# A diffusion transformer block on one core: ten of its sixteen MLP batches taken in pairs, with wider matmuls

## The chip, the cores and the metric

The kernel runs on 1 core of a Trainium2 chip. The metric is device time in microseconds (us) of one execution. Three executions were timed and one further execution was profiled. In the profile the engines are PE (matmul, with its weight loads shown apart as PEld), DVE, ACT and POOL; SP issues DMAs.

## The reference

One block with self-attention, cross-attention and an MLP over 16 batches of 256 tokens with 256 features. What the change touches is the end, the MLP (cut to it):

```python
        x = x + c_attn_out
        x_norm2 = modulate(_ln(x), shift_m, scale_m)
        h = jax.nn.gelu(x_norm2 @ W_mlp1 + b_mlp1)
        h = h @ W_mlp2 + b_mlp2
        x = x + gate_m[:, None] * h
        return x
```

The scale, shift and gate differ from batch to batch; the two weight matrices (256 x 1024 and 1024 x 256) are the same for all.

## The kernel before

The attention of all batches comes first, and takes the span's first three quarters. It stores each batch's stream to a DRAM buffer, `x2d`. The MLP follows, with the first batches' preparation already laid into the end of the attention.

**Precision.** Each f32 operand of a product is split into a high part (type fp32r) and a low part, high and low being `hi` and `lo`, or `hh` and `hl`. A product is three matmuls for each slice of 128 in the contraction: high by high, high by low, low by high (`mm3`, `mm3_tok`).

**A batch's preparation.** `mlp_load` fetches the batch from `x2d` (SP). `mlp_bias` adds a row on POOL (`x<-x,cb`). `mlp_stats` takes mean and variance on DVE (`st_m`, `mv_m`, `rs_m`) and raises to the power -1/2 on POOL (`rs_m<-rs_m,mhalf`). `mlp_apply` normalizes on DVE, in two halves (`xn_m`). Below these three together are the norm. `mlp_T` is the turn: PE transposes `xn_m` into PSUM (`psT_m`, four transposes), DVE scales and shifts it (`xTf_m`), ACT makes `hi` (or a DVE copy, for the batches in the list `'DV'`), and DVE makes `lo`. `mlp_residual` fetches the gate rows (`gm`) and adds one to the stream on DVE (`xmg`).

**A chunk.** The 1024 hidden features are taken 256 at a time, so a batch has four chunks (b, 0) to (b, 3). A chunk is three stages. `mlp_first` (lines 747 to 758) is the first product into one PSUM bank (`ph`): two slices of 128 features, each six matmuls with 256 moving columns, the batch's tokens. `mlp_gelu` (760 to 773) reads that bank on ACT, twice for each half: `hf` in f32 and `hh` in fp32r; POOL subtracts them into `hl`. `mlp_second` (775 to 789) multiplies by W2 into the bank pair `sp` or `st`, 12 matmuls with 256 moving columns. With the last chunk it ends the batch: DVE multiplies both halves by the gate (`mt`), adds the residual (`y`), and SP stores.

**The order.** It is written out by hand in the loop from line 1122. At chunk i the program issues gelu of chunk i+1, the turn of a batch if one is due, the first product of chunk i+2, the second product of chunk i-1, then the norm, residual or load that is due. PE, DVE, POOL and SP keep the program's order, each as its own queue; ACT does so up to chunk `'AP'`, 23, and the built order is the program's after it too. Before the change, batch b+1 is turned at (b, 0), batch b+2 is normed at (b, 1), the residual of batch b is taken at (b, 2), and batch b+3 is loaded at (b, 3). The first two chunk positions of the loop are special and not touched.

Buffers: `hh` and `hl` have three each, `ph` two, `x` five, `xn` three.

Of the kernel before, what the change touches and what calls it, by code (L numbers as in the profile page):

```python
# [21 lines left out]
def pixart_block(  # L22
# [8 lines left out]
    B, N, H = x.shape  # L31
# [3 lines left out]
    NT = N // P  # L35
    KC = H // P
    MLP = W_mlp1.shape[1]
    NF = MLP // P
# [13 lines left out]
                return tc.keep_in_program_order(i) if self.on else i  # L52
            return issue

    E_ = {'M': ((-17, -12, -10, -1, 1), (0, 3, 4, 7, 9), (8, 11, 13, 15)), 'CUT': 8, 'LN': {'s': 'pool', 'c': 'pool', 'q': 'pool'}, 'ON': (1, 1, 1), 'L0': -16, 'L1': 1, 'S0': -7, 'A0': 0, 'T0': 1, 'H': (7, 11, 14, 15), 'S1': 5, 'A1': 7, 'L2': 9, 'T1': 9, 'S2': 32, 'AP': 23, 'DV': (0, 1), 'HP': (1, 0), 'BZ': {}, 'AV': {1: [(1, 2), (1, 3)], 9: [(0, 0), (0, 1)]}, 'AHEAD': (0, 0, 0, 0, 0, 2), 'W1P': [(-9, 1), (-8, 1), (-7, 1), (-6, 1), (-5, 1), (-5, 5), (-4, 1), (-4, 3), (-4, 5), (-3, 1), (-3, 3), (-3, 5), (-2, 1)], 'W2P': [(-4, 7), (-3, 0), (-3, 4), (-3, 6), (-3, 7), (-2, 2), (-2, 4), (-2, 6), (-1, 0), (-1, 1)], 'XP': 1, 'IL': 1, 'MF': 0, 'SH': 4, 'RAMP': 1, 'HA': 1, 'MP': 16, 'W': (7, 1, 0, 0), 'PRE': 'z0qp z0kp load rest ld2 one0 silu b12 brow L0a turn L0b b4 L0d scale T0t sc1 hik lok T0h T0l b4 shift b4 hiq L1a L1b bk loq K0a K0b K0x0 K0x1 K0y0p K0y1p L1d T1t K0l T1h K0l0 K0l1 Q0a Q0m bq Q0h Q0x0 Q0y0p Q0x1 Q0y1p T1l Q0l Q0l0 Q0l1 z1kp z1qp K1a K1b hiv lov Q1a Q1b K1x0 K1x1 K1y0 K1y1 K1l K1l0 K1l1 Q1x0 Q1x1 Q1y0 Q1y1 Q1l Q1l0 Q1l1 L2a L2b L2c V0a V0b bv b5 ld3', 'SL': {(-1, 0): 'V1a', (-1, 1): 'T2t T2h T2p vone z2kp z2qp', (-1, 2): 'V1b', (-1, 3): 'rest', (-1,4): 'M0 rest one1 ld4', (-1, 5): 'K2a L3a', (-1, 6): 'K2m L3b L3p L3c', (-1, 7): 'd3 one2 rest', (0, 0): 'd6 rest', (0, 1): 'rest', (0, 2): 'd3', (0, 4): 'rest', (1, 0): 'rest', (1, 2): 'rest', (1, 4): 'rest', (30, 0): 'd3', (30, 1): 'd2', (30, 2): 'd3', (30, 5): 'd3', (31, 1): 'd2'}}

    PE = InOrder(nc.tensor, True)
    ACT, DVE, POOL, SP = (InOrder(e, True) for e in (nc.scalar, nc.vector, nc.gpsimd, nc.sync))

    const = ctx.enter_context(tc.tile_pool(name="const", bufs=1))  # L60
    work = ctx.enter_context(tc.tile_pool(name="work", bufs=2))
# [23 lines left out]
    big = [const.tile([P, 2, 8, N], F32R, name=f"big{i}") for i in range(3)]  # L85
# [6 lines left out]
    BMOD, BQKV, BQC, BKVC, BM1 = 0, 12, 18, 20, 24  # L92
# [5 lines left out]
    def tok(ap, b):  # L98
        return ap[b].rearrange("(t p) h -> p t h", p=P)
# [5 lines left out]
    brow = const.tile([32, P], F32, name="brow")  # L105
# [20 lines left out]
    sc1 = const.tile([P, 2, 2, B], F32, name="sc1")  # L126
    bT = const.tile([P, 32], F32, name="bT")
# [5 lines left out]
    st = psum.tile([P, 2, 512], F32, tag="st", name="st", bufs=1)  # L133
    sp = psum.tile([P, 2, 512], F32, tag="s", name="s", bufs=1)
# [35 lines left out]
    ts = [work.tile([P, 2, KC, H], F32, tag="pt", name=f"wf{i}", bufs=5) for i in range(3)]  # L170
# [552 lines left out]
    def mlp_T(b):  # L723

        m = M[b]
        pst = ps_gen(f"psT_m{b}", SHORT)
        for f in range(KC):
            for t in range(NT):
                PE.transpose(pst[:, f * N + t * P:f * N + (t + 1) * P],
                             m.ln.xn[:, t, f * P:(f + 1) * P], ident)  # L730
        y = work.tile([P, KC, N], F32, tag="y", name=f"xTf_m{b}", bufs=2)
        hi, lo = (Wkc, Wqc)[b % 2]
        for f in range(KC):
            DVE.tensor_scalar(y[:, f], pst[:, f * N:(f + 1) * N], sc1[:, 1, f, b:b + 1],
                              cpT[:, 6 + f, b:b + 1], ALU.mult, ALU.add)
# [24 lines left out]
    def mlp_gelu(b, c):  # L760
        ph = M[b].h.pop(c)
        hf = work.tile([P, 2, N], F32, tag="pt", name=f"hf_{b}_{c}", bufs=5)
        hh = work.tile([P, 2, N], F32R, tag="qkh", name=f"hh_{b}_{c}", bufs=3)
        hl = work.tile([P, 2, N], F32R, tag="qkl", name=f"hl_{b}_{c}", bufs=3)
        for dst in (hf, hh):
            if b == 0:
                ACT.activation(dst, ph, AF.Gelu_apprx_tanh)
                continue
            for j in range(2):
                f = BM1 + 2 * c + j  # L770
                ACT.activation(dst[:, j], ph[:, j], AF.Gelu_apprx_tanh, bias=bT[:, f:f + 1])
        POOL.tensor_tensor(hl, hf, hh, ALU.subtract)
        M[b].hT[c] = (hh, hl)

    def mlp_second(b, c):
        m = M[b]
        hT = m.hT.pop(c)
        if c == 0:
            m.po = [(sp, st)[b % 2][:, t, :H] for t in range(NT)]
        for t in range(NT):  # L780
            mm3_tok(m.po[t], hT, t, [W2[0][:, 2 * c:2 * c + 2], W2[1][:, 2 * c:2 * c + 2]],
                    kn=2, start=(c == 0), stop=(c == NCH - 1))
        if c == NCH - 1:
            t1 = work.tile([P, NT, H], F32, tag="t1", name=f"mt_{b}")
            for t in range(NT):
                DVE.tensor_tensor(t1[:, t], m.po[t], m.g[:, 0], ALU.mult)
            y = work.tile([P, NT, H], F32, tag="x1", name=f"y_{b}", bufs=5)
            DVE.tensor_tensor(y, m.xg, t1, ALU.add)
            SP.dma_start(tok(out, b), y)


    W1P, W2P = E_['W1P'], E_['W2P']
    W1 = [wself[:, 8 * i:8 * i + 8].rearrange("p (k c) h -> p k (c h)", k=KC) for i in range(2)]
    W2 = [big[2][:, 0], big[2][:, 1]]
# [301 lines left out]
    for n in range(-1, nu):  # L1096
        ACT.on = E_['ON'][0] or n >= nu - 1
        for k in range(8):
# [7 lines left out]
            for q in (2 * k, 2 * k + 1):  # L1106
# [6 lines left out]
    pst = iter([lambda: o.turn(1), lambda: o.norm(1),  # L1113
                lambda: (o.aT.turn(), o.aT.high()), o.aT.low,
                lambda: o.proj(0), lambda: o.proj(1), lambda: (o.end(), o.add(), o.store())])
    chunks = [(b, c) for b in range(B) for c in range(NCH)]
    mlp_first(*chunks[4])
    mlp_gelu(*chunks[0])
    next(pst)()
    mlp_first(*chunks[5])  # L1120
    next(pst)()
    for i, (b, c) in enumerate(chunks):
        ACT.on = i < E_['AP']
        if i + 1 < len(chunks):
            mlp_gelu(*chunks[i + 1])
        if c == 0 and 0 < b < B - 1:
            mlp_T(b + 1)
        if i > 3 and i + 2 < len(chunks):
            mlp_first(*chunks[i + 2])
        if i > 0:  # L1130
            mlp_second(*chunks[i - 1])
        for _, f in zip(range(1), pst):
            f()
        if c == 1 and 2 < b + 2 < B:
            mlp_bias(b + 2)
            mlp_stats(b + 2)
            mlp_apply(b + 2)
        if c == 2:
            mlp_residual(b)
        if c == 3 and b + 3 < B:  # L1140
            mlp_load(b + 3)
    mlp_second(*chunks[-1])


# [46 lines left out]
```

## Time and profile before

| what | value |
|---|---|
| median of three runs | 805.61 us (803.01 to 806.17) |
| the profiled execution | 804.78 us |
| its span, first to last instruction | 803.0 us |
| PE, PEld busy | 97%, 82% |
| DVE, ACT, POOL busy | 74%, 73%, 58% |
| granted clock of PE | 1.0 |
| matmuls | 9455 |

The first row is the time that counts; the second is the execution from which every duration here is taken. Busy shares are over the whole span. A PE that is busy 97% has little room, but matmuls overlap in the pipeline: the distance between starts tells what one costs, not its duration. In a timeline row the columns are the start in us, the length in us, the engine, the line, the operation with output and inputs, the count, and in brackets the idle time before it with what ended that. In a row of waits they are the engine that waited and its tile, what it waited for, the total in us, the number of times, and the longest. All instructions carry line 51, that of a recording helper, so one goes by the tiles' names.

### The profile page before, as it was taken

The numbers are of one execution on the slowest core, as the hardware profiler recorded it, in microseconds if no ns is written. First come the engines' busy times: TensorE is split into PE (matmuls) and PEld (weight loads), VectorE is DVE, ScalarE is ACT, GpSimd is POOL, SyncE is SP. The second block draws the span as 40 slices with busy tenths as digits, with TensorE's granted clock in tenths as the row PEclk, the third lists the DMA queues.
The fourth block names the chain that finished last, engine by engine and source line by source line (L and its number), as shares of the span: only waits on it lengthen the run. The fifth ranks groups of instructions, "written<-read, shape, count | busy, mean of one in ns | idle before, by whom it ended". The sixth has DMA issues, their size and how long they took to land.

```text
span 803.0 us, 23712 instructions
## 1 busy us (share of the span) xinstructions
PE 781.8 (97%) x9455; PEld 660.3 (82%) x9455; DVE 596.0 (74%) x1063; ACT 584.8 (73%) x1024; POOL 465.4 (58%) x405
## 2 busy tenths in 40 slices
PE   9999999999999999999999999999899999999997
PEld 8677777887887877878788788777669999999997
DVE  4787878888888888878887888777674656666662
ACT  3377887888887888878888788877666666666663
POOL 5745837475564647456364767654446666666653
PEclk9999999999999999999999999999999999999999
DMA  6553444345353444535444454534311322212211
GB/s 189 147 172 95 133 113 123 100 120 146 95 147 104 137 107 123 146 94 146 113 132 130 137 151 120 148 101 129 106 42 42 92 60 60 80 58 62 80 43 51
DMA packets 89938, 87.88 MB, mean 109 GB/s; under 512 B 9506, under 2 KB 85572, under 8 KB 89828
## 3 DMA queue, kind: packets, MB, share of 16 engines
q1 hardware_dynamic: 89364, 85.58, 37.7%
q8 instruction: 75, 1.23, 0.7%
q0 software_dynamic: 192, 0.52, 0.2%
q14 instruction: 35, 0.29, 0.1%
q10 hardware_dynamic: 272, 0.26, 0.1%
HBM read 26.97 MB, written 8.46 MB: 44 GB/s over the span
## 4 chain that ended last, share of the span: by engine, by line
PE 79%; DVE 9%; ACT 4%; POOL 3%; issue 3%; DMA 1%; ACTq 0%; POOLq 0%; SPq 0%
PE s L51 17%; PE o L51 14%; PE ph L51 11%; PE st L51 11%; DVE mx L51 7%; PE ps_qc L51 3%; PE ps_kc L51 3%; PE ps_q L51 3%; ACT pt L51 2%; PE ps_P_s L51 2%; PE ps_v_s L51 2%; PE ps_v_c L51 2%; PE psm L51 2%; PE ps_k L51 1%; PE ps_P_c L51 1%
## 5 line engine op out<-in xcount | busy, mean ns | idle before, releaser
L51 DVE TENSOR_REDUCE mx<-s 128x4 f32<-128x1024 f32 (+1 forms) x267 | 309.2, 1163 | 94.6 <-PE s L51 92.0
L51 ACT ACTIVATE pt<-st 128x1024 f32<-128x1024 f32 x252 | 257.0, 1020 | 40.3 <-PE st L51 34.1
L51 PE MATMUL s<-big 63*128 63x256 f32 (+1 forms) x1024 | 122.1, 309 | 6.5 <-DVE mx L51 3.6
L51 PE MATMUL o<-pt,v 128*32 128x256 f32 x2048 | 123.8, 382 | 0.0
L51 POOL TENSOR_TENSOR hl<-hf,hh 128x512 fp32r<-128x512 f32 x64 | 88.7, 1396 | 55.0 <-ACT hh L51 54.0
L51 PEld LDWEIGHTS s<-big 63*128 63x128 f32 (+1 forms) x1024 | 81.2, 185 | 41.6 <-DVE mx L51 19.0
L51 PE MATMUL st<-big 64*128 64x256 f32 (+1 forms) x1024 | 108.8, 284 | 4.9 <-ACT pt L51 4.9
L51 PEld LDWEIGHTS o<-pt,v 128*32 128x32 f32 x2048 | 60.0, 109 | 40.8
L51 PEld LDWEIGHTS st<-big 64*128 64x128 f32 (+1 forms) x1024 | 82.1, 186 | 9.3 <-ACT pt L51 7.5
L51 ACT ACTIVATE hf<-ph,bT 128x256 f32<-128x256 f32 x120 | 50.6, 474 | 27.8 <-PE ph L51 27.8
L51 ACT COPY oT<-o 128x512 f32<-128x512 f32 x63 | 37.0, 587 | 42.5 <-PE o L51 42.5
L51 ACT ACTIVATE hh<-ph,bT 128x256 fp32r<-128x256 f32 x120 | 50.5, 472 | 23.8 <-PE s L51 12.0
L51 POOL TENSOR_TENSOR xTl_c<-y_c,xTh_c 128x512 fp32r<-128x512 f32 x16 | 20.5, 1282 | 61.6 <-PE s L51 52.3
L51 POOL TENSOR_TENSOR xTl_as<-y_as,xTh_as 128x512 fp32r<-128x512 f32 x16 | 20.5, 1279 | 56.4 <-ACT y_as L51 56.4
L51 PE MATMUL ph<-wqch,wself 128*128 128x256 f32 x256 | 51.8, 285 | 0.0
L51 PE MATMUL ph<-wkch,wself 128*128 128x256 f32 x256 | 51.8, 286 | 0.0
L51 POOL TENSOR_TENSOR xTl_ac<-y_ac,xTh_ac 128x512 fp32r<-128x512 f32 x16 | 20.6, 1284 | 52.8 <-ACT y_ac L51 48.8
L51 PE MATMUL s<-big,hh 128*128 128x256 f32 x256 | 47.4, 282 | 0.0
L51 PE MATMUL st<-big,hh 128*128 128x256 f32 x256 | 47.2, 281 | 0.0
L51 DVE TENSOR_SCALAR xn_m<-x,mv_m,rs_m 128x256 f32<-128x256 f32 x32 | 38.4, 1238 | 11.4 <-POOL rs_m L51 11.4
L51 PEld LDWEIGHTS ph<-wqch,wself 128*128 128x128 f32 x256 | 42.0, 191 | 0.4 <-issue 0.4
L51 PEld LDWEIGHTS ph<-wkch,wself 128*128 128x128 f32 x256 | 41.9, 191 | 0.4
(223 smaller groups left out, 2381.0 us busy)
## 6 DMA issues: line engine op xcount, KB each, us to landing
big<-h_kc SPq DMA_DIRECT2D x64, 128.0 KB
big<-h_qc SPq DMA_DIRECT2D x64, 128.0 KB
big<-h_k SPq DMA_DIRECT2D x62, 128.0 KB
big<-h_q SPq DMA_DIRECT2D x62, 128.0 KB
big<-l_k SPq DMA_DIRECT2D x32, 128.0 KB
big<-l_q SPq DMA_DIRECT2D x32, 128.0 KB
c<-in_ctx_dram SPq DMA_DIRECT2D x16, 256.0 KB
g<-gd SPq DMA_DIRECT2D x16, 256.0 KB
```

The lines of the kernel that those rows point to most:

```text
L51: i = f(*a, **k)
```

## The change

Batches 4 to 13 become five pairs (4,5) to (12,13). A pair's `hi` and `lo` lie side by side in a part of `big[0]`, a tile that the attention has left by then, so that one matmul moves 512 columns, the tokens of both batches. A pair has eight chunks of 128 features, labelled (2p, 0) to (2p+1, 3): six wide matmuls, two gelu operations of 512 columns, one subtraction, and 12 matmuls of the second product, 256 columns each as before. Both batches of a pair end together, after its eighth chunk. The other batches keep their functions.

The preparation is moved: pairs turn batch v+2 at (v, 0), norm batch v+3 at (v, 1) and load batch v+4 at (v, 3). Between single batches and pairs the order is listed: norm 3 at (1, 1), 4 at (1, 3), 5 at (2, 1); turn 3 at (2, 0), 4 at (2, 2), 5 at (3, 0). The `hi` of batches 3, 4 and 5 is made on DVE. The last batch ends in two halves of 128 tokens, each multiplied, added and stored by itself. Which of `sp` and `st` a batch or pair accumulates in is chosen anew.

```diff
-    'DV': (0, 1)
+    'DV': (0, 1, 3, 4, 5)
...
         hi, lo = (Wkc, Wqc)[b % 2]
+        if 3 < b < B - 2:
+            q = b // 2 % 2
+            m.pair = [big[0][:, i, 4 * q:4 * q + 4].rearrange("p (k e) n -> p k (e n)", k=KC)
+                      for i in range(2)]
+            hi, lo = [w[:, :, b % 2 * N:b % 2 * N + N] for w in m.pair]
...
+    def mlp_end(b, ts=(slice(0, NT),)):
+        m = M[b]
+        t1 = work.tile([P, NT, H], F32, tag="t1", name=f"mt_{b}")
+        y = work.tile([P, NT, H], F32, tag="x1", name=f"y_{b}", bufs=5)
+        for s in ts:
+            for t in range(NT)[s]:
+                DVE.tensor_tensor(t1[:, t], m.po[t], m.g[:, 0], ALU.mult)
+            DVE.tensor_tensor(y[:, s], m.xg[:, s], t1[:, s], ALU.add)
+            SP.dma_start(tok(out, b)[:, s], y[:, s])
+
+    def two_first(p, f):
+        ph = ps_gen(f"ph2_{p}_{f}", LONG)
+        xT = M[2 * p + 1].pair
+        n = 0
+        for k in range(KC):
+            for a, b in ((0, 0), (0, 1), (1, 0)):
+                PE.matmul(ph, W1[a][:, k, f * P:(f + 1) * P], xT[b][:, k], start=(n == 0), stop=(n == 3 * KC - 1))
+                n += 1
+        M[2 * p].h[f] = ph
+
+    def two_gelu(p, f):
...
+        for dst in (hf, hh):
+            ACT.activation(dst.rearrange("p e n -> p (e n)"), ph, AF.Gelu_apprx_tanh,
+                           bias=bT[:, BM1 + f:BM1 + f + 1])
+        POOL.tensor_tensor(hl, hf, hh, ALU.subtract)
+
+    def two_second(p, f):
+        hT = M[2 * p].hT.pop(f)
+        for e in range(2):
...
+            for t in range(NT):
+                for n, (a, b) in enumerate(((0, 0), (0, 1), (1, 0))):
+                    PE.matmul(m.po[t], hT[a][:, e, t * P:(t + 1) * P], W2[b][:, f],
...
+        if f == NF - 1:
+            mlp_end(2 * p)
+            mlp_end(2 * p + 1)
...
+    chunks = [single(b, c) for b in range(4) for c in range(NCH)]
+    chunks += [double(p, f) for p in range(2, B // 2 - 1) for f in range(NF)]
+    chunks += [single(b, c) for b in range(B - 2, B) for c in range(NCH)]
+    turns = {(1, 0): [2], (2, 0): [3], (2, 2): [4], (3, 0): [5]}
+    norms = {(1, 1): [3], (1, 3): [4], (2, 1): [5]}
+    loads = {(0, 3): [3], (1, 0): [4], (1, 2): [5]}
+    for v in range(4, B - 2):
+        turns[v, 0] = [v + 2]
+    for v in range(3, B - 3):
+        norms[v, 1] = [v + 3]
+    for v in range(2, B - 4):
+        loads[v, 3] = [v + 4]
```

More of the change, by code (lines that the diff above doesn't have):

```diff
@@ L53, in __getattr__ @@
             return issue
-    E_ = {'M': ((-17, -12, -10, -1, 1), (0, 3, 4, 7, 9), (8, 11, 13, 15)), 'CUT': 8, 'LN': {'s': 'pool', 'c': 'pool', 'q': 'pool'}, 'ON': (1, 1, 1), 'L0': -16, 'L1': 1, 'S0': -7, 'A0': 0, 'T0': 1, 'H': (7, 11, 14, 15), 'S1': 5, 'A1': 7, 'L2': 9, 'T1': 9, 'S2': 32, 'AP': 23, 'DV': (0, 1), 'HP': (1, 0), 'BZ': {}, 'AV': {1: [(1, 2), (1, 3)], 9: [(0, 0), (0, 1)]}, 'AHEAD': (0, 0, 0, 0, 0, 2), 'W1P': [(-9, 1), (-8, 1), (-7, 1), (-6, 1), (-5, 1), (-5, 5), (-4, 1), (-4, 3), (-4, 5), (-3, 1), (-3, 3), (-3, 5), (-2, 1)], 'W2P': [(-4, 7), (-3, 0), (-3, 4), (-3, 6), (-3, 7), (-2, 2), (-2, 4), (-2, 6), (-1, 0), (-1, 1)], 'XP': 1, 'IL': 1, 'MF': 0, 'SH': 4, 'RAMP': 1, 'HA': 1, 'MP': 16, 'W': (7, 1, 0, 0), 'PRE': 'z0qp z0kp load rest ld2 one0 silu b12 brow L0a turn L0b b4 L0d scale T0t sc1 hik lok T0h T0l b4 shift b4 hiq L1a L1b bk loq K0a K0b K0x0 K0x1 K0y0p K0y1p L1d T1t K0l T1h K0l0 K0l1 Q0a Q0m bq Q0h Q0x0 Q0y0p Q0x1 Q0y1p T1l Q0l Q0l0 Q0l1 z1kp z1qp K1a K1b hiv lov Q1a Q1b K1x0 K1x1 K1y0 K1y1 K1l K1l0 K1l1 Q1x0 Q1x1 Q1y0 Q1y1 Q1l Q1l0 Q1l1 L2a L2b L2c V0a V0b bv b5 ld3', 'SL': {(-1, 0): 'V1a', (-1, 1): 'T2t T2h T2p vone z2kp z2qp', (-1, 2): 'V1b', (-1, 3): 'rest', (-1,4): 'M0 rest one1 ld4', (-1, 5): 'K2a L3a', (-1, 6): 'K2m L3b L3p L3c', (-1, 7): 'd3 one2 rest', (0, 0): 'd6 rest', (0, 1): 'rest', (0, 2): 'd3', (0, 4): 'rest', (1, 0): 'rest', (1, 2): 'rest', (1, 4): 'rest', (30, 0): 'd3', (30, 1): 'd2', (30, 2): 'd3', (30, 5): 'd3', (31, 1): 'd2'}}
@@ new lines, in pixart_block @@
+    E_ = {'M': ((-17, -12, -10, -1, 1), (0, 3, 4, 7, 9), (8, 11, 13, 15)), 'CUT': 8, 'LN': {'s': 'pool', 'c': 'pool', 'q': 'pool'}, 'ON': (1, 1, 1), 'L0': -16, 'L1': 1, 'S0': -7, 'A0': 0, 'T0': 1, 'H': (7, 11, 14, 15), 'S1': 5, 'A1': 7, 'L2': 9, 'T1': 9, 'S2': 32, 'AP': 23, 'DV': (0, 1, 3, 4, 5), 'HP': (1, 0), 'BZ': {}, 'AV': {1: [(1, 2), (1, 3)], 9: [(0, 0), (0, 1)]}, 'AHEAD': (0, 0, 0, 0, 0, 2), 'W1P': [(-9, 1), (-8, 1), (-7, 1), (-6, 1), (-5, 1), (-5, 5), (-4, 1), (-4, 3), (-4, 5), (-3, 1), (-3, 3), (-3, 5), (-2, 1)], 'W2P': [(-4, 7), (-3, 0), (-3, 4), (-3, 6), (-3, 7), (-2, 2), (-2, 4), (-2, 6), (-1, 0), (-1, 1)], 'XP': 1, 'IL': 1, 'MF': 0, 'SH': 4, 'RAMP': 1, 'HA': 1, 'MP': 16, 'W': (7, 1, 0, 0), 'PRE': 'z0qp z0kp load rest ld2 one0 silu b12 brow L0a turn L0b b4 L0d scale T0t sc1 hik lok T0h T0l b4 shift b4 hiq L1a L1b bk loq K0a K0b K0x0 K0x1 K0y0p K0y1p L1d T1t K0l T1h K0l0 K0l1 Q0a Q0m bq Q0h Q0x0 Q0y0p Q0x1 Q0y1p T1l Q0l Q0l0 Q0l1 z1kp z1qp K1a K1b hiv lov Q1a Q1b K1x0 K1x1 K1y0 K1y1 K1l K1l0 K1l1 Q1x0 Q1x1 Q1y0 Q1y1 Q1l Q1l0 Q1l1 L2a L2b L2c V0a V0b bv b5 ld3', 'SL': {(-1, 0): 'V1a', (-1, 1): 'T2t T2h T2p vone z2kp z2qp', (-1, 2): 'V1b', (-1, 3): 'rest', (-1,4): 'M0 rest one1 ld4', (-1, 5): 'K2a L3a', (-1, 6): 'K2m L3b L3p L3c', (-1, 7): 'd3 one2 rest', (0, 0): 'd6 rest', (0, 1): 'rest', (0, 2): 'd3', (0, 4): 'rest', (1, 0): 'rest', (1, 2): 'rest', (1, 4): 'rest', (30, 0): 'd3', (30, 1): 'd2', (30, 2): 'd3', (30, 5): 'd3', (31, 1): 'd2'}}
@@ L778, in mlp_second @@
         if c == 0:
-            m.po = [(sp, st)[b % 2][:, t, :H] for t in range(NT)]
+            m.po = [(sp, st)[(b + b // (B - 2)) % 2][:, t, :H] for t in range(NT)]
         for t in range(NT):
@@ L783, in mlp_second @@
         if c == NCH - 1:
-            t1 = work.tile([P, NT, H], F32, tag="t1", name=f"mt_{b}")
-            for t in range(NT):
[L786 to L789, printed above, removed]
+            mlp_end(b, [slice(t, t + 1) for t in range(NT)] if b == B - 1 else (slice(0, NT),))
+    def mlp_end(b, ts=(slice(0, NT),)):
[7 more added lines that the diff above has]
+            SP.dma_start(tok(out, b)[:, s], y[:, s])
@@ new lines, in two_first @@
+    def two_first(p, f):
[8 more added lines that the diff above has]
+    def two_gelu(p, f):
+        ph = M[2 * p].h.pop(f)
+        hf = work.tile([P, 2, N], F32, tag="pt", name=f"hf2_{p}_{f}", bufs=5)
+        hh = work.tile([P, 2, N], F32R, tag="qkh", name=f"hh2_{p}_{f}", bufs=3)
+        hl = work.tile([P, 2, N], F32R, tag="qkl", name=f"hl2_{p}_{f}", bufs=3)
+        for dst in (hf, hh):
+            ACT.activation(dst.rearrange("p e n -> p (e n)"), ph, AF.Gelu_apprx_tanh,
+                           bias=bT[:, BM1 + f:BM1 + f + 1])
+        POOL.tensor_tensor(hl, hf, hh, ALU.subtract)
+        M[2 * p].hT[f] = (hh, hl)
@@ new lines, in two_second @@
+    def two_second(p, f):
+        hT = M[2 * p].hT.pop(f)
+        for e in range(2):
+            m = M[2 * p + e]
+            if f == 0:
+                m.po = [(sp, st)[p % 2][:, e, t * H:(t + 1) * H] for t in range(NT)]
+            for t in range(NT):
+                for n, (a, b) in enumerate(((0, 0), (0, 1), (1, 0))):
+                    PE.matmul(m.po[t], hT[a][:, e, t * P:(t + 1) * P], W2[b][:, f],
+                              start=(f == t == n == 0), stop=(f == NF - 1 and t == NT - 1 and n == 2),
+                              skip_group_check=True)
+        if f == NF - 1:
+            mlp_end(2 * p)
+            mlp_end(2 * p + 1)
@@ L1115, in pixart_block, with single, double, do @@
                 lambda: o.proj(0), lambda: o.proj(1), lambda: (o.end(), o.add(), o.store())])
-    chunks = [(b, c) for b in range(B) for c in range(NCH)]
-    mlp_first(*chunks[4])
-    mlp_gelu(*chunks[0])
+    def single(b, c):
+        return b, c, mlp_first, mlp_gelu, mlp_second, (b, c)
+    def double(p, f):
+        return 2 * p + f // 4, f % 4, two_first, two_gelu, two_second, (p, f)
+    chunks = [single(b, c) for b in range(4) for c in range(NCH)]
[10 more added lines that the diff above has]
+        loads[v, 3] = [v + 4]
+    def do(stage, i):
+        chunks[i][2 + stage](*chunks[i][5])
+    do(0, 4)
+    do(1, 0)
     next(pst)()
-    mlp_first(*chunks[5])
+    do(0, 5)
     next(pst)()
-    for i, (b, c) in enumerate(chunks):
+    for i, (b, c, *_) in enumerate(chunks):
         ACT.on = i < E_['AP']
         if i + 1 < len(chunks):
-            mlp_gelu(*chunks[i + 1])
-        if c == 0 and 0 < b < B - 1:
-            mlp_T(b + 1)
+            do(1, i + 1)
+        for v in turns.get((b, c), ()):
+            mlp_T(v)
         if i > 3 and i + 2 < len(chunks):
-            mlp_first(*chunks[i + 2])
+            do(0, i + 2)
         if i > 0:
-            mlp_second(*chunks[i - 1])
+            do(2, i - 1)
         for _, f in zip(range(1), pst):
             f()
[L1134 to L1137, printed above, removed]
+        for v in norms.get((b, c), ()):
+            mlp_bias(v)
+            mlp_stats(v)
+            mlp_apply(v)
         if c == 2:
             mlp_residual(b)
-        if c == 3 and b + 3 < B:
-            mlp_load(b + 3)
-    mlp_second(*chunks[-1])
+        for v in loads.get((b, c), ()):
+            mlp_load(v)
+    do(2, len(chunks) - 1)
 _P = 'L0_xcond_'
```

## Prediction, made before the changed kernel was run

> **What bounds the kernel now.** I read the page's list of engines first (PE 97% of the span), then a table of stretches over the MLP, since an average over stages says nothing about the one that is changed.
>
> ```profile
> core 0: us, PE busy (x) PEld busy (x) DVE busy (x) ACT busy (x) POOL busy (x), PEclk, DMA share, GB/s
> 660.00:680.00 20.00, 20.00 (x168) 19.59 (x167) 12.14 (x23) 12.59 (x30) 13.19 (x11) 1.00 0.28 79
> ```
>
> PE and its weight loads are full; DVE, ACT and POOL are 60 to 66% busy. So only a shorter PE queue helps here, and other engines count where PE waits for one of them. The chain of waits ends in an unbroken run of the second product, and the PE timeline gives the price of a matmul.
>
> ```profile
> 792.29 5.76 PE st L51 x48
> ```
> ```profile
> 706.67 0.28 PE L51 MATMUL ph<-wkch,wself 128*128 128x256 f32 x1
> ...
> 709.54 0.28 PE L51 MATMUL ph<-wqch,wself 128*128 128x256 f32 x1
> ...
> 712.41 0.28 PE L51 MATMUL ph<-wqch,wself 128*128 128x256 f32 x1
> ```
>
> A chunk (12 matmuls of each product) takes 2.87 us, so a matmul with 256 moving columns takes 2.87/24 = 119.5 ns (the durations of 0.28 overlap). The one other thing on PE is the turn of the next batch, four transposes, which waits:
>
> ```profile
> PEld psT_m L51 <- DVE xn_m L51: 2.9, 13, 0.4
> ```
>
> The last two timelines, DVE and POOL around one turn (first transpose at 715.28), tell why.
>
> ```profile
> 707.67 0.69 DVE L51 TENSOR_TENSOR y<-xmg,mt 128x512 f32<-128x512 f32 x1
> 710.80 0.75 DVE L51 BATCH_NORM_STATS2 st_m<-x 128x6 f32<-128x256 f32 x2 [2.44 <-POOL x L51]
> ...
> 712.79 2.67 DVE L51 TENSOR_SCALAR xn_m<-x,mv_m,rs_m 128x256 f32<-128x256 f32 x2 [0.82 <-POOL rs_m L51]
> ```
> ```profile
> 707.79 1.72 POOL L51 TENSOR_TENSOR hl<-hf,hh 128x512 fp32r<-128x512 f32 x1 [2.19 <-ACT hh L51]
> 709.47 1.29 POOL L51 TENSOR_TENSOR x<-x,cb 128x512 f32<-128x512 f32 x1
> 712.05 0.70 POOL L51 TENSOR_TENSOR rs_m<-rs_m,mhalf 128x2 f32<-128x2 f32 x1 [1.29 <-DVE rs_m L51]
> 712.72 2.59 POOL L51 TENSOR_TENSOR hl<-hf,hh 128x512 fp32r<-128x512 f32 x2
> ```
>
> hl takes 1.29 alone but 1.72 when y began first: y ends at 708.36, and 708.36 + 1.29 is 0.14 more than hl's end. The two xn take 2.67, ending 0.15 after the two hl beside them; with POOL idle, two took 0.73 at 596.57. So these DVE and POOL operations exclude each other, whichever began first. The norm is thus a chain of fixed length: from the start of chunk (b,1) at 706.67 to the end of xn at 715.46 is 8.8 us, against 3 x 2.87 = 8.6 to the turn. The turn's second transpose waits about 0.13 per batch.
>
> **First product: fewer, wider matmuls.** The order of the changed program shows 8 x 6 matmuls of 512 columns for each of 5 pairs: 240 replace 480. No row has 512 moving columns in this type. The low end is 215 ns, from plain f32 matmuls with 256 moving columns and only 16 stationary ones. I read them as moving each column in twice the time of an fp32r one, which is as long as 512 fp32r columns:
>
> ```profile
> 591.56 0.81 PE L51 MATMUL ps_gm<-wgm,sT 128*16 128x256 f32 x3
> ```
>
> (0.81 - 0.38 for the last one's length)/2 = 215. The high end is twice 119.5 = 239. The weight load of 0.19 begins as the matmul before it begins, so behind 215 of streaming it is hidden; I take 217, near the row that streams as long. Saving 240 x (239 - 217) = **5.3 us** (0 to 5.8). A pair chunk becomes 2.87 - 6 x 0.022 = 2.74. The second product keeps its matmul count. ACT's four gelu of 256 become two of 512: 4 x 0.42 (they start 0.37 apart) against 2 x 0.63 (rows hf and hh from hk), free time on an engine that is 63% busy.
>
> The Trainium skill's page "TensorE: Matmul & The Clock Gate", section "Back-to-back issue gap", gives about 131 ns per matmul of 512 columns in a stream of loads and matmuls, and 216 isolated. The row of 215 speaks for the second; by the first the saving would be 240 x 108 = 26 us.
>
> **Steady state, turns of batches 7 to 15.** Turns still lie three chunks after their norm, now 3 x 2.74 = 8.2 us, while the norm's chain doesn't shrink as much. Measured from the start of chunk (b,1): gelu's hh waits for the second product (0.14) and takes 0.63, so hl begins at 0.90 instead of 1.12. Odd b, no end of a batch before it: hl to 2.2, x+cb 3.4, statistics 4.65, power 5.4, two hl with xn 8.1: no wait. Even b: both batches of a pair end here, DVE has two mt (0.76), y, two mt, y. The first y wants to begin at 1.0 and finds hl holding; y 2.0 to 2.7; x+cb 2.6 to 3.9; second y to 4.4; statistics to 5.6, power 6.4, xn to 9.1. The second transpose could go at 8.3, so PE waits 0.86. That is turns 9, 11, 13, 15; turn 7 follows one batch's end: 0.3. Together 3.75, against 10 x 0.13 = 1.3 for turns 6 to 15 now: **+2.5 us** (-1.3 if no norm is late, +2.5 as worked out).
>
> The rule against this change is the skill's page "SBUF — State Buffer", section "Who interferes with whom": a DVE instruction with two SBUF inputs contends with a GpSimd one that reads SBUF, and whoever issues first blocks the other for the whole instruction. The rows above agree (1.72 against 1.29; 2.67 against 0.73).
>
> **The passage from single batches to pairs.** Pair (4,5) needs both turned by chunk (3,2), so norms 4 and 5 move up to (1,3) and (2,1), and DVE's queue holds norm 4 ahead of turn 3's copies. What is queued behind each wait: POOL's power of norm b holds back the hl of following chunks; DVE's xn holds xTf, hi, lo, and PE waits for lo. With durations of the profile (x+cb and hl 1.29, statistics to rs 1.2, power 0.8 with its gaps, xn 2.7 when POOL runs beside, xTf 1.0, hi copy 0.43, lo 0.69, mt and y 1.45): norm 3 ends at 630.84 as now. x4+cb runs 630.7 to 632.0 and xmg_1 waits for it to 632.5; statistics to 633.7, power 634.5, xn_4 to 637.2. xTf_3 to 638.25, hi behind x5+cb 638.7, lo_3 639.4: PE was ready for it at 637.7, **1.8** lost (and 0.15 at turn 4). End of batch 1 to 640.9, statistics 5 to 642.1, power 642.9, xn_5 645.7; turn 5 waits **0.5**. xTf_4, hi, lo with an hl between, 648.45; xmg_2 649.2; xTf_5, hi, lo with two POOL operations between, 653.2; PE is ready at 651.9: **1.35**. End of batch 2, norm 6 to 659.35; turn 6 waits **0.75**. Sum 4.55, less 0.27 that turns 4 and 5 wait now: 4.3. If POOL loses each race, xn takes 0.73, 1.9 less each, and nothing is left: -0.3. I take **+3.5**, near the upper end, since thirteen turns in the row above do wait for xn. The three hi copies moved from ACT to DVE are in this chain.
>
> **Last batch in halves.** Now mt, mt, y take 0.76 + 0.69 after PE. The changed DVE order is mt, y, mt, y with one PE wait ahead: about 4 x 0.42, so the last store starts 0.2 later but carries 128 KB, not 256. An estimate: **-0.3** (-0.6 to +0.3). Loads and gate rows come a batch earlier or in the same place; SP is idle most of the time and no wait for x<-x2d shows among these stages, so nothing. If a load came late, its norm would be late by as much.
>
> **Sum** against the profiled execution (804.78 us, span 803.0, 1.8 around it): 804.78 - 5.3 + 2.5 + 3.5 - 0.3 = **805.2**. The median of the three runs is 805.61, 0.8 above that execution, so no change within what they scatter (803.01 to 806.17). About 0.5%, 4.0 us, is what a measurement can tell from no change.
>
> **Rivals.**
> 1. The cover holds: DVE and POOL keep pace and turns wait no longer than now. For it: both are idle a third of the time. Against it: the fixed chain of 8.8 us. 804.78 - 5.3 - 0.3 = 799.2. Chance 0.20.
> 2. Wide matmuls cost what two narrow ones do (239 ns), because what makes 119.5 grows with the columns and isn't the weight load. Then the passage still costs 4.3; chunks stay 2.87, so even turns wait 0.5 and odd none: 4 x 0.5 - 1.3 = +0.7; tail -0.3: 809.5, slower. It decides from about 234 ns on. For it: the plain f32 warming matmuls (wz), 128 by 128, load as long (0.19) and start 0.11 apart, so the load alone needn't be what costs 119.5. Chance 0.17.
> 3. The program doesn't do what it says: the order of its instructions has the 240 wide matmuls, so no chance is left for this.
>
> Forecast 0.63. The range leaves about 0.1 on either side: 799.5 to 809.0. Faster by over 0.5%: rival 1, 0.20. Slower: rival 2, 0.17. Within: 0.63.
>
> **What would show it.** Right: ph2 matmuls start 215 to 220 ns apart; turns of odd batches from 9 wait 0.8, even ones not at all; the chunk (2,2) holds a stall of over 1 us behind lo_3; xn still takes 2.7 in most batches. Wrong: wide matmuls at 235 or more, or at 130; turns that don't wait; a passage that costs under 1 us, which would mean that the exclusion of DVE and POOL is misread.

## The result, and the profile after

The changed kernel takes 806.65 us (median, 804.96 to 808.71), the kernel before 803.94 us on the same chips (802.44 to 807.79): ratio 1.003, 95% interval 1.002 to 1.0039. It is slower, by 2.7 us; the forecast was 805.2 and no change. The profiled execution took 807.52 us, with a span of 805.4.

From the page after, the busy shares, and the group of the wide matmuls (busy us, mean ns of one, idle time before it and its releaser).

```profile
PE 779.9 (97%) x9215; PEld 647.9 (80%) x9215; DVE 608.3 (76%) x1067; ACT 569.6 (71%) x938; POOL 462.9 (57%) x405
...
L51 PE MATMUL ph<-big,wself 128*128 128x512 f32 x240 | 63.4, 398 | 1.1 <-DVE big L51 1.1
```

There are 240 matmuls fewer, and PE is busy 1.9 us less. The 398 ns of a wide matmul is its length, not its price; that is the distance from one start to the next. A timeline of PE, one pair chunk:

```profile
686.23 1.55 PE L51 MATMUL ph<-big,wself 128*128 128x512 f32 x6
687.62 0.40 PE L51 MATMUL st<-big,hh 128*128 128x256 f32 x2
```

Six wide matmuls and the change to the next product take 687.62 - 686.23 = 1.39 us, 232 ns each. In the single starts of the trace the spacing in the pairs is 232.5, from 229 to 237 by the place in the chunk. A pair chunk is 2.83 us, not 2.74.

What PE's weight loads wait for from 585 us on (columns: total us, times, longest); before, the first of these rows had 2.9, 13, 0.4, and the three on `ph` were not there:

```profile
PEld psT_m L51 <- DVE xn_m L51: 3.2, 7, 0.5
PEld ph L51 <- DVE big L51: 1.4, 1, 1.4
...
PEld ph L51 <- ACT hh L51: 1.2, 1, 1.2
...
PEld ph L51 <- DVE wqcl L51: 0.5, 1, 0.5
```

Thirteen small waits for `xn` have become seven larger ones, and two stalls for a turn's copies have come in. The first row on `ph` is the stall for batch 5. On DVE, the `hi` copy of batch 5 is held by POOL (1.24 for 0.43), its `lo` by POOL's x+cb (1.66 for 0.69).

```profile
649.45 0.99 DVE L51 TENSOR_SCALAR xTf_m<-psT_m,sc,cpT 128x256 f32<-128x256 f32 x2
650.48 1.24 DVE L51 CAST big<-xTf_m 128x512 fp32r<-128x512 f32 x1
651.75 1.66 DVE L51 TENSOR_TENSOR big<-xTf_m,big 128x512 fp32r<-128x512 f32 x1
```

And on PE, where the first wide matmul (with `hi`) goes at 651.90 and the second (with `lo`) waits for DVE:

```profile
651.90 0.43 PE L51 MATMUL ph<-big,wself 128*128 128x512 f32 x1
653.46 1.43 PE L51 MATMUL ph<-big,wself 128*128 128x512 f32 x5 [1.13 <-DVE big L51]
```

The other two rows are one stall, for the copies of batch 3. DVE's `lo` ends at 639.75, since `xn_4` holds the copies until 637.54:

```profile
634.94 2.67 DVE L51 TENSOR_SCALAR xn_m<-x,mv_m,rs_m 128x256 f32<-128x256 f32 x2 [0.81 <-POOL rs_m L51]
637.54 0.98 DVE L51 TENSOR_SCALAR xTf_m<-psT_m,sc,cpT 128x256 f32<-128x256 f32 x2
638.56 0.47 DVE L51 CAST wqch<-xTf_m 128x512 fp32r<-128x512 f32 x1
639.06 0.69 DVE L51 TENSOR_TENSOR wqcl<-xTf_m,wqch 128x512 fp32r<-128x512 f32 x1
```

PE waits first for `hi` (`wqch`, done at 639.03), then for `lo` (`wqcl`). Its weight loads wait 1.2 and 0.5 us there, 1.6 together before rounding; the profile puts the first down to ACT's `hh`, but the matmul starts as `hi` is done:

```profile
639.17 0.36 PE L51 MATMUL ph<-wqch,wself 128*128 128x256 f32 x1 [0.95 <-DVE wqch L51]
639.81 0.38 PE L51 MATMUL ph<-wqcl,wself 128*128 128x256 f32 x1 [0.28 <-DVE wqcl L51]
```

**The account.** I take the stretch from the first transpose of batch 2's turn to the start of the last matmul, which holds all of the change but its tail. It was 618.50 to 797.77 = 179.27 us and is 619.03 to 800.52 = 181.49: +2.2. The tail, from that matmul's start to the end of the span, was 5.2 (802.95 - 797.77) and is 4.9 (805.39 - 800.52): -0.3. All that lies before batch 2's turn is the same code in both; there the execution after is 0.5 us later.

### The profile page after: what moved, and what is told of

It reads as the page before. It is cut to its first block, busy times and chain, and to the rows that moved or that the text cites. A ratio compares the mean times of both kernels' runs of the same rounds, so it can differ in the third digit from the quotient of the medians.

```text
span 805.4 us, 23144 instructions
## 1 busy us (share of the span) xinstructions
PE 779.9 (97%) x9215; PEld 647.9 (80%) x9215; DVE 608.3 (76%) x1067; ACT 569.6 (71%) x938; POOL 462.9 (57%) x405
## 4 chain that ended last, share of the span: by engine, by line
PE 70%; DVE 13%; ACT 5%; POOL 5%; issue 5%; DMA 2%; SPq 0%; ACTq 0%; POOLq 0%
PE s L51 15%; PE o L51 14%; PE st L51 8%; DVE mx L51 8%; PE ph L51 7%; PE ps_q L51 3%; PE ps_qc L51 3%; ACT pt L51 3%; PE ps_kc L51 3%; PE ps_k L51 2%; DVE xn_m L51 2%; PE ps_P_s L51 2%; PE psm L51 2%; PE ps_v_s L51 1%; PE ps_v_c L51 1%
## 5 line engine op out<-in xcount | busy, mean ns | idle before, releaser
L51 POOL TENSOR_TENSOR hl<-hf,hh 128x512 fp32r<-128x512 f32 x64 | 84.1, 1323 | 53.3 <-ACT hh L51 53.1
L51 ACT ACTIVATE hf<-ph,bT 128x256 f32<-128x256 f32 (+1 forms) x80 | 44.3, 580 | 38.6 <-PE ph L51 38.6
L51 ACT ACTIVATE hh<-ph,bT 128x256 fp32r<-128x256 f32 (+1 forms) x80 | 44.4, 581 | 30.7 <-PE s L51 14.8
L51 PE MATMUL ph<-big,wself 128*128 128x512 f32 x240 | 63.4, 398 | 1.1 <-DVE big L51 1.1
L51 PE MATMUL s<-big,hh 128*128 128x256 f32 x288 | 53.2, 282 | 0.0
L51 PEld LDWEIGHTS ph<-big,wself 128*128 128x128 f32 x240 | 42.2, 188 | 8.4 <-DVE big L51 1.4
L51 PEld LDWEIGHTS s<-big,hh 128*128 128x128 f32 x288 | 45.9, 189 | 1.9
L51 PE MATMUL st<-big,hh 128*128 128x256 f32 x224 | 41.4, 282 | 0.0
L51 PE MATMUL s<-big,hl 128*128 128x256 f32 x144 | 40.5, 281 | 0.0
```

Of the source, the lines that this page charges most:

```text
L51: i = f(*a, **k)
```

## The experiments

**Theory A**, from the traces: the wide matmuls give 1.6 us and not 5.3; the order of the preparation costs 3.2 at the passage and 0.6 in the turns, since DVE and POOL exclude each other and DVE's queue is in order. **Its rivals**: the pairs themselves are slow (wide matmuls, gelu on a full bank, two batches ending at once); or DVE simply has too much to do, and a stall that is removed comes back elsewhere.

All ratios are against runs of the kernel before on the same chip. x1 to x4 ran on one chip, x6 to x9 on a second, x10 to x12 on a third and x13 on a fourth, so times are compared only within a group. "The stretch" is the one above, from each run's own profiled execution.

| run | ratio (95% interval) | stretch, us |
|---|---|---|
| before | 1 | 179.3 |
| the change | 1.003 (1.002 to 1.0039) | 181.5 |
| x1_narrow | 1.0048 (1.0031 to 1.0066) | 185.0 |
| x2_tail | 0.9989 (0.9975 to 1.0004) | 179.3 |
| x3_order | 1.0055 (1.0037 to 1.0072) | 183.3 |
| x4_actnorm | 1.0121 (1.0095 to 1.0148) | 189.8 |
| x6_hl_dve | 0.9997 (0.9983 to 1.001) | 178.4 |
| x7_early | 1.0056 (1.0039 to 1.0073) | 182.4 |
| x8_both | 0.9989 (0.997 to 1.0007) | 177.4 |
| x9_before_hl | 0.9963 (0.9944 to 0.9982) | 176.6 |
| x12_best | 0.9957 (0.9941 to 0.9972) | 179.7 |
| x13_hi_act | 0.9982 (0.9963 to 1.0001) | 178.5 |

The stretches of x4_actnorm, x7_early and x12_best each hold one dip of the granted clock to 0.50 for 3.4 us, worth some 1.7 us by estimate (last section). x10_load64 and x11_quarters have one time each, given below.

### What a wide matmul costs: x1_narrow, x10_load64, x11_quarters

x1_narrow, the changed kernel with two halves for each wide matmul:

```diff
-                PE.matmul(ph, W1[a][:, k, f * P:(f + 1) * P], xT[b][:, k], ...)
+                for e in range(2):
+                    PE.matmul(ph[:, e * N:(e + 1) * N], W1[a][:, k, f * P:(f + 1) * P],
+                              xT[b][:, k, e * N:(e + 1) * N], ...)
```

> The changed kernel, but each wide matmul of the pairs' first product is issued as two of 256 columns with the same stationary block. Theory A (the wide matmul is worth what its spacing says, 239.0 for two narrow ones less 232.5 ns for one wide): 240 x 6.5 ns = 1.6 us come back, pair chunks are 2.87 us again instead of 2.83, so the chain of the norm waits 0.5 us less in all (odd turns 0.35 instead of 0.46): about 1.1 us slower than the changed kernel, some 3.4 to 3.8 us over the kernel before, ratio 1.004 to 1.005. Theory B (the slow-down sits in the wide matmuls or in the gelu and subtraction that hang on a wide bank, so that narrow ones repair it): at or under the kernel before. Theory C (the spacing in the trace misleads, a wide matmul is worth the 5.3 us of the prediction): 5 us over the changed kernel, ratio about 1.010.

Its ratio lies in theory A's range, though the interval overlaps that of the changed kernel; the traces decide. The stretch grew by 3.5 us, not 1.1, so that the ratio fits is partly luck. The matmuls are 119.5 ns apart again, 1.6 us in all. The other 1.9 are turns, which wait more in total:

```profile
PEld psT_m L51 <- DVE xn_m L51: 5.3, 11, 1.1
```

The odd turns from 9 on wait 0.36 us each, as I had forecast with the longer chunk. What I had missed are turns 7, 8 and 12, with about 1.2, 0.2 and 0.9. Ahead of turn 12 an `hl` began on POOL at 720.62 and `xmg` on DVE at 720.70, and `xmg` took 1.77 us; one batch on, `xmg` began 0.08 before its `hl` and took 0.68. Which of DVE and POOL goes first thus changes with small shifts, and the sum of durations does not give it.

x10_load64 halves the stationary block, with the moving width at 512. It leaves out half of the hidden features of the pairs; gelu, `hl` and the second product use 64 partitions too (not shown):

```diff
-                PE.matmul(ph, W1[a][:, k, f * P:(f + 1) * P], xT[b][:, k], ...)
+                PE.matmul(ph[:64], W1[a][:, k, f * P:f * P + 64], xT[b][:, k], ...)
```

> The changed kernel with only 64 of each 128 hidden features in the pairs: stationary blocks of 64 columns in the first product, 64 partitions in gelu, subtraction and second product; half of the hidden features of batches 4 to 13 are left out. The moving width stays 512. It asks why a wide matmul takes 232.5 ns and not 217. Theory A (the moving columns set the pace): the spacing of the wide matmuls stays at 230 to 235 ns. Theory B (the load of 128 stationary columns, 188 ns, gets in the way of the stream): loads take about half as long and the spacing falls to about 217 ns. The time itself says little: 1.6 us of spacing at most.

Its loads, then its matmuls, in one chunk each:

```profile
718.48 1.11 PEld L51 LDWEIGHTS ph<-big,wself 128*64 128x64 f32 x6
```

```profile
718.49 1.60 PE L51 MATMUL ph<-big,wself 128*64 128x512 f32 x6
```

A load takes 134 ns (188 to 192 for 128 columns), and the starts of the wide matmuls are still 234 ns apart (median in the trace). Theory A: at 512 columns the moving columns set the pace, and a shorter load does not change it. Its time, 815.99 us in one run, has another cause, told at the end.

x11_quarters issues each wide matmul as four of 128 columns (as x1_narrow, with `range(4)` and slices of `P`).

> The changed kernel with each wide matmul issued as four of 128 moving columns, same stationary block each time. It asks for the price of a matmul at a third width. Theory A (each column 0.44 ns and some 6.5 ns fixed, from 119.5 at 256 and 232.5 at 512): 63 ns apart, if a load of 188 ns can be issued that often; four of them 252 ns, so 240 x 20 ns = 4.7 us over the changed kernel. Theory B (a load has a price of its own that cannot be hidden behind 128 columns): 90 to 120 ns apart, four of them 360 to 480, 30 to 60 us over the changed kernel.

```profile
715.85 2.79 PE L51 MATMUL ph<-big,wself 128*128 128x128 f32 x24
718.48 0.45 PE L51 MATMUL st<-big,hh 128*128 128x256 f32 x2
```

(718.48 - 715.85)/24 = 110 ns; the run took 855.47 us, and its stretch of 229.9 us is 48 longer than the changed kernel's. Theory B holds at this width: with a load for each, these matmuls are 110 ns apart, where theory A had 63. That the load sets this floor was not varied. So the three widths are 110, 119.5 and 232.5 ns. The last two give (232.5 - 119.5)/256 = 0.44 ns a column, an estimate by which 256 columns take 113 of the 119.5 ns: the product already ran near its column rate, and doubling the width saves 3%.

### Where the rest came from: x3_order, x2_tail

x3_order keeps the change's order, buffers, DVE copies and tail, and takes every batch alone:

```diff
-    chunks = [single(b, c) for b in range(4) for c in range(NCH)]
-    chunks += [double(p, f) for p in range(2, B // 2 - 1) for f in range(NF)]
-    chunks += [single(b, c) for b in range(B - 2, B) for c in range(NCH)]
+    chunks = [single(b, c) for b in range(B) for c in range(NCH)]
```

> The changed kernel's order of preparation, its buffers, its copies on DVE and its last batch in halves, but every batch goes through the first product alone, in four chunks, as before. Theory A (the passage costs): norms 4 and 5 ahead of time still hold back the copies of turns 3 to 5, so PE loses some 3.3 us between batches 2 and 4 as in the changed kernel; later turns wait 0.13 each as before; tail -0.35. Some 2.5 to 3 us over the kernel before, ratio 1.003 to 1.004. Theory B (what the changed kernel lost comes with the pairs, in wide matmuls and in the end of two batches at once): within 0.5 us of the kernel before, ratio 0.9995 to 1.0005.

Theory A, and more than it said: the stretch is 4.0 us over that of before. The order alone costs more than the whole change; the pairs give 1.8 back (183.3 - 181.5), about the 1.6 of their matmuls. The stall for the copies of batch 3 is the same in this run (1.0 and 0.3 us in PE's waits). That for batch 5 is gone, because alone it is needed later, but turns 6 and 7 wait 1.7 and 1.0 us instead, so the pairs' 1.8 is a sum in which waits differ too.

x2_tail, the kernel before with the last batch in halves:

```diff
-            y = work.tile([P, NT, H], F32, tag="x1", name=f"y_{b}", bufs=5)
-            DVE.tensor_tensor(y, m.xg, t1, ALU.add)
-            SP.dma_start(tok(out, b), y)
+            for s in [slice(t, t + 1) for t in range(NT)] if b == B - 1 else [slice(0, NT)]:
+                for t in range(NT)[s]:
+                    DVE.tensor_tensor(t1[:, t], m.po[t], m.g[:, 0], ALU.mult)
+                DVE.tensor_tensor(y[:, s], m.xg[:, s], t1[:, s], ALU.add)
+                SP.dma_start(tok(out, b)[:, s], y[:, s])
```

> The kernel before with only the last batch added and stored in halves. Theory A: the stretch from the last matmul to the end shrinks by 0.35 us, as between the two traces (5.23 against 4.88 us): ratio 0.9996. Theory B (the shorter tail of the changed kernel is chance): no difference, 1.0000; the two can be told apart in the trace's tail, hardly in the time.

Its tail is 802.06 - 797.19 = 4.9 us against 5.2: theory A in the trace (by the unrounded spans it is 0.3, not 0.35). The ratio's interval takes in 1.

### Taking the cause of the waits away: x4_actnorm, x6_hl_dve, x9_before_hl

x4_actnorm normalizes on ACT, one chunk later (and keeps ACT in the program's order after chunk 23 too, `'AP'` 99):

```diff
-        M[b].ln.steps[2]("dve")
+        M[b].ln.steps[2]("dve" if b < 3 else "act")
```

> The changed kernel, with the normalization of batches 3 to 15 taken from DVE to ACT, issued one chunk later behind the gelu of that chunk, so that it no longer shares DVE's and POOL's mutual exclusion. Theory A (turn waits and passage come from DVE and POOL excluding each other and from DVE's order): the waits of odd turns (4 x 0.46 us) go, the passage loses part of its 3.3 us, since xn no longer stands ahead of the copies of the turn: 2 to 4 us faster than the changed kernel, at or just under the kernel before, ratio 0.998 to 1.001. Theory B (turn waits come from the length of the chain, not from the exclusion): the normalization merely moves behind gelu on ACT, turns wait as long or longer, 0 to 3 us slower than the changed kernel, ratio 1.003 to 1.007.

Both theories missed the size: 1.2% slower. The dip in its stretch is only 1.7 us of that stretch's 8.4 over the changed kernel. ACT is the engine that empties `ph`, and `xn` stands ahead of gelu in its queue:

```profile
PE ph L51 <- ACT hh L51: 6.1, 9, 0.9
PE psT_m L51 <- ACT xn_m L51: 2.0, 4, 1.1
```

So this run tells only that ACT is the wrong place, and nothing on the exclusion.

x6_hl_dve leaves `xn` on DVE and takes away what POOL does beside it:

```diff
+        due = norms.get(chunks[i - 1][:2], ()) if i else ()
         if i + 1 < len(chunks):
+            hl_on[0] = DVE if due else POOL
             do(1, i + 1)
+        for v in due:
+            mlp_apply(v)
```

(`hl` is issued on `hl_on[0]`, and the norm's own place keeps only x+cb and the statistics. On DVE nothing but this `hl` comes between statistics and `xn` by it.)

> The changed kernel; in the one chunk after each norm's statistics the subtraction hl is made on DVE instead of POOL, ahead of the normalization. POOL then has nothing that holds off xn (2.7 us for two halves beside two hl, 0.7 alone). Theory A (waiting turns and part of the passage are the exclusion of DVE and POOL): xn ends 0.6 to 1.9 us earlier; the waits of turns 9, 11, 13, 15 (4 x 0.46) and those of turns 3, 6 and 7 (0.7 together) go; lo of batch 3 comes earlier, so that about 1 us of its 1.6 goes; lo of batch 5 stays late. 3 to 4 us faster than the changed kernel, 0.3 to 1 under the kernel before, ratio 0.998 to 1.000. Theory B (DVE's queue is the limit): hl now stands in DVE's queue, the second product waits for it, and the time stays at 1.002 to 1.005.

Theory A in the trace; the ratio lies in its range and its interval takes in 1. DVE in the steady state, around the turn of batch 9, which waited 0.46 us in the changed kernel:

```profile
691.39 0.69 DVE L51 TENSOR_TENSOR hl<-hf,hh 128x512 fp32r<-128x512 f32 x1
692.68 1.69 DVE L51 TENSOR_SCALAR xn_m<-x,mv_m,rs_m 128x256 f32<-128x256 f32 x2 [0.60 <-POOL rs_m L51]
```

`xn` takes 1.69 us where it took 2.66; from turn 6 on, every turn comes 11.75 to 11.81 us after the one before it, where the changed kernel has 11.75 and 12.27 alternately. What is left of PE's waits on preparation is the passage:

```profile
PEld ph L51 <- DVE big L51: 1.4, 1, 1.4
PEld psT_m L51 <- DVE xn_m L51: 1.0, 1, 1.0
PEld ph L51 <- DVE wqcl L51: 0.9, 1, 0.9
```

Against my expectation, batch 3 gains nothing: its turn waits 0.9 us and its `lo` another 1.0, against 0.4 and 1.6; why, no run tells. The stretch is 3.1 us shorter than the changed kernel's.

x9_before_hl gives the same edit, and the tail in halves, to the kernel before. `due` is there `c == 2 and 2 < b + 2 < B`.

> The kernel before, with hl on DVE after a norm and with the last batch in halves, without pairs. Theory A: its 13 turns wait 0.13 us each at xn, which goes: -1.7, with the tail -0.35: 2 us under the kernel before, ratio 0.9975. The pairs by themselves are then worth the 1.6 us of their matmuls or less. Theory B: these 0.13 us are not a wait for xn, ratio 0.9996.

The stretch is 2.6 us shorter than before, where I expected 1.7: the distance of two turns falls from 12.08 to 12.11 to an even 11.91 us, so the waits had cost 0.18 a batch and not 0.13. In its profile no wait of PE for `xn` is left from 585 us on. It is faster than the kernel before and than the change, without pairs.

### The passage: x7_early, x8_both, x12_best, x13_hi_act

x7_early moves three norms, loads and turns:

```diff
-    turns = {(1, 0): [2], (2, 0): [3], (2, 2): [4], (3, 0): [5]}
-    norms = {(1, 1): [3], (1, 3): [4], (2, 1): [5]}
-    loads = {(0, 3): [3], (1, 0): [4], (1, 2): [5]}
+    turns = {(1, 0): [2], (1, 3): [3], (2, 1): [4], (2, 3): [5]}
+    norms = {(1, 0): [3], (1, 2): [4], (2, 0): [5]}
+    loads = {(0, 2): [3], (0, 3): [4], (1, 1): [5]}
```

> The changed kernel; loads, norms and turns of batches 3, 4 and 5 all one chunk earlier, nothing else. Theory A (the passage is late because these three norms come too close to their use): lo of batches 3 and 5 come in time, 1.6 and 1.35 us saved, turn waits as they are: about 3 us faster than the changed kernel, ratio 0.999 to 1.001. Theory B (what is late is DVE's total of work in this stretch, two batches more in the time of one): the stalls only move by a chunk, ratio stays at 1.002 to 1.004.

Theory B, with a reservation. No wait for a copy is left, but the turns of batches 3 and 5, moved with their norms, wait about 2 and 1.2 us: the stalls moved. The stretch is 0.9 us longer than the change's, but holds a dip of the clock worth some 1.7 us, right after the stall at turn 3; without it, the stretch would be 0.8 shorter, where theory A had 3. Another 1.5 us of that execution lies before batch 2's turn, where the code is the same. In the times the edit saves nothing.

x8_both joins x6_hl_dve and x7_early.

> Both edits, hl on DVE after a norm and the passage one chunk earlier. If the two are independent as theory A has it: 5 to 6 us faster than the changed kernel; what is left of the change is then 1.6 us by wider matmuls, 0.35 by the tail and 1.3 by turns that no longer wait: about 2.5 to 3 us under the kernel before, ratio 0.9965. Theory B: no better than the better one of the two alone.

Its stretch is 4.1 us shorter than the change's, more than either alone and less than the 5 to 6 of theory A; the time shows it less clearly, a ratio of 0.9989 whose interval takes in 1. One stall is left, at the turn of batch 3, 2.3 us:

```profile
PEld psT_m L51 <- issue: 1.7, 2, 1.3
...
PEld psT_m L51 <- DVE xn_m L51: 1.1, 1, 1.1
```

x12_best is x8_both with the `turns` of the changed kernel.

> The changed kernel with hl on DVE after a norm, with norms and loads of batches 3, 4 and 5 one chunk earlier, and with the turns where the changed kernel has them (the run with both edits lost 2.3 us at the turn of batch 3 alone, which came one chunk earlier there too). Theory A (all that stood against the pairs was preparation that comes late): no stall of over 0.3 us is left in the MLP; 2.3 us off that run: 4 us under the kernel before, 1.5 under the kernel before with hl on DVE and the tail in halves; ratio 0.9945 to 0.9955. Theory B (the stall goes to the turn of batch 4 or 5, since DVE has no room): as that run, ratio 0.998 to 0.999.

The time says theory A: 801.54 us against 805.21, ratio 0.9957, faster than both kernels of this case. The profile does not confirm it step by step. That execution, 804.76 us, is the longest of its seven. The stall at batch 3's turn is gone; turn 5 waits 0.5 and turn 7 about 2.3 us, and the dip of the clock follows. DVE is late there. As I read its rows, the gate rows arrive late and POOL's `hl` then holds `xmg` (1.80 us for 0.69); no run tests this:

```profile
655.88 1.80 DVE L51 TENSOR_TENSOR xmg<-x,gm 128x512 f32<-128x512 f32 x1 [0.85 <-DMA gm<-gd]
657.60 0.98 DVE L51 TENSOR_SCALAR xTf_m<-psT_m,sc,cpT 128x256 f32<-128x256 f32 x2
```

Whether the other executions have that stall stays open. For the passage the second rival, that DVE has too much to do, is therefore not ruled out: whenever a stall was taken away there, another came up elsewhere. Nor is it shown that the pairs are worth having: x9_before_hl, with the same edit and no pairs, has the ratio 0.9963, and the intervals overlap. The traces of both show a batch every 11.75 us with pairs and 11.91 without, 1.6 us over ten batches.

x13_hi_act undoes one more part of the change, in x12_best:

```diff
-    'DV': (0, 1, 3, 4, 5)
+    'DV': (0, 1)
```

> As the last version (hl on DVE after a norm, norms and loads of batches 3, 4, 5 one chunk earlier, turns where the changed kernel has them), and hi of batches 3, 4 and 5 made on ACT as in the kernel before, not on DVE. In the last version the profile still shows PE waiting 0.5 us at turn 5 and about 2.3 us at turn 7, and xTf of batch 6 two microseconds later after its turn than in the steady state. Theory A (DVE is 2 us behind there with work, and its three hi copies of 0.43 us alone, 0.43 to 1.1 beside POOL, are part of that): the waits shrink by 1 to 2 us together, ratio 0.994 to 0.995. Theory B (DVE is not behind for want of time; it is held up by the order of its queue and by POOL, and a hi made on ACT behind gelu comes later than on DVE): the waits stay or grow, ratio 0.996 to 0.998.

Nearer theory B: 0.9982. The waits at turns 5 and 7 are gone, but 3.4 us of waits for `ph` have come in. On ACT `hi` waits for DVE's `xTf`, and gelu waits behind it in ACT's queue, so `ph` is not emptied:

```profile
638.87 1.02 ACT L51 ACTIVATE wqch<-psT_m,cpT,sc 128x256 fp32r<-128x256 f32 x2 [4.59 <-DVE xTf_m L51]
639.79 0.84 ACT L51 ACTIVATE hf<-ph,bT 128x256 f32<-128x256 f32 x2
```

```profile
PEld ph L51 <- ACT hh L51: 3.4, 2, 1.9
```

That the three copies on DVE paid is likely and not shown: the interval of this run overlaps that of x12_best, and the stretches differ little, 178.5 us against 179.7 with a dip of 1.7 in it.

## Why the prediction was wrong

| step | predicted | measured in the traces |
|---|---|---|
| wide matmuls | -5.3 | 240 x (239.0 - 232.5) = -1.6 |
| steady turns 7 to 15 | +2.5 | +0.6 |
| passage to pairs | +3.5 | 1.6 + 0.15 + 1.4 + 0.3 - 0.27 = +3.2 |
| last batch in halves | -0.3 | -0.3 |
| sum | +0.4 | +1.9 |

- **The step that failed is the size of the wide matmul:** "I take 217, near the row that streams as long". It is 232.5. The row was one of plain f32, 256 moving and 16 stationary columns, and I read its 215 ns as the streaming time of 512 fp32r columns. That reading was not tested by any row, and it was off by 15 ns, 3.7 us in 240. Both bounds, 215 and 239, held. The better row was at hand: if 119.5 is mostly columns, 512 cost nearly twice that. Rival 2 said so ("what makes 119.5 grows with the columns and isn't the weight load"). x10_load64 shows it at 512 columns; for 256 it follows by the estimate of 113 in 119.5. The prediction gave that rival 0.17.
- **The Trainium skill's rule** cited there, "TensorE: Matmul & The Clock Gate", section "Back-to-back issue gap", has 131 ns for 512 columns in a stream and 216 isolated. In this type, with a load for each, 232.5 was measured: above both, and the measurement decides.
- **The steady turns** were right in kind and place: odd turns from 9 on wait, even ones do not, turn 7 hardly (0.05). The size was 0.46 each, not 0.86. The chunk accounts for 0.27 of that: three chunks are 8.49 us, not 8.22; the norm's chain itself came within 0.1 us of what was worked out (`xn` ends 9.0 us after the chunk's start, 686.23 to 695.23). That the exclusion of DVE and POOL makes these waits is shown by x6_hl_dve, where they go. (Of the two rows that the prediction set beside the rule on two SBUF inputs, the one of `xn` is no case of it: `xn` reads one tile and a pair of numbers a row. It is held off all the same.) What they were worth in the kernel before was set too low: 0.18 a batch by x9_before_hl, where I had 0.13.
- **The passage** was right in its two largest places (1.8 at the copies of batch 3, measured 1.6; 1.35 at `lo` of batch 5, measured 1.4), the turns of batches 5 and 6 too large (0.5 and 0.75, measured 0.15 and 0.3). That the sum is near is partly luck: the places worked out gave 4.3, and the 3.5 was a choice below it in case POOL lost some races. x3_order shows that it belongs to the order, not to the pairs.
- **The tail** was right, and x2_tail shows it alone.
- The sum misses by 1.5 us; another 0.5 lies before batch 2's turn, in code that is the same, and the profiled execution has 0.3 more around its span. That makes 805.2 into 807.5.

The range (799.5 to 809.0) holds the time. The forecast of no change failed by the one term: with 232.5 in the prediction's own sum it would have been 804.8 - 1.6 + 2.5 + 3.5 - 0.3 = 808.9, slower.

## What to carry to other kernels

Price a wider matmul by asking what sets the spacing now: if the narrow one is already near its column rate (here 113 of 119.5 ns), widening saves only the few ns that are left. Where several batches must be prepared early, look at the order of the queues ahead of the first use; here that order cost 3.2 us, twice what the wide matmuls gave. When an engine's operation takes three times its length beside another's, try moving the neighbour in that one chunk, not the operation itself: one `hl` in four on DVE was worth 2.6 us in the kernel before, more than all the wide matmuls.

## What the runs showed of the hardware

- Spacing of fp32r matmuls with their own 128-column load: 110 ns at 128 moving columns, 119.5 at 256, 232.5 at 512.
- In x10_load64 the change from the wide matmuls (blocks of 128 rows by 64 columns) to the second product (64 rows) takes 326 ns from start to start and back 206, against 237 and 114 in the changed kernel: about 90 ns more at each change. The spacing after it is longer too, 223 against 118 and 285 against 235. Together that is 0.32 us a chunk, 13 us in 40 chunks, which is the 11.1 by which its stretch (192.6) exceeds the changed kernel's and the turns' waits of some 2 us that the longer chunk takes away. The Trainium skill, "TensorEngine Tiling (Array Packing)", section "Key Properties", says that a change of tiling mode drains the engine; the extra time at each change fits that, but no run here shows a drain as its cause.
- The granted clock falls to about 0.50 for a short spell after a stretch in which PE idled. Each pair of rows has the 3.4 us before a dip and the dip itself, in the profiled executions of x7_early, x12_best and x4_actnorm (stretch, length, PE busy, PEclk, DMA share, GB/s):

```profile
629.18:632.59 3.41, 1.79 (x14) 1.00 0.27 93
632.59:636.00 3.41, 3.41 (x18) 0.50 0.00 0
```
```profile
666.59:670.00 3.41, 1.50 (x9) 1.00 0.41 142
670.00:673.42 3.42, 3.42 (x14) 0.50 0.28 77
```
```profile
645.73:649.14 3.41, 1.81 (x12) 1.00 0.01 3
649.14:652.55 3.41, 3.41 (x19) 0.50 0.00 0
```

Half the clock for 3.4 us of full work loses some 1.7 us, an estimate. So a stall may cost more than its own length. That the idling brings the dip on is a reading that no run tests: in the changed kernel the stall for batch 3 left PE 2.19 us busy of 3.42 (637.68 to 641.10) and no dip followed, while in x8_both a dip of 6.8 us, to 0.52, followed 2.54 busy of 3.42, at 55.85 us, and its MLP begins some 3 us late.
- In x9_before_hl POOL's power of two numbers a row takes 1.08 us when DVE's `hl` runs beside it, against 0.70 in the kernel before, with DVE idle: a tiny operation is held off as a large one is.
